# Edge values of raw patch sets moved to GpSimd, and a root spread by a matmul, at the start of a two-layer lookup convolution

## The chip, the cores and the metric

The kernel runs on one core of one Trainium2 chip. The metric is the device time of one execution in microseconds (us), lower is better; the time of a kernel is the median of its runs. Engines are named as in the profile: PE is TensorE (matmuls; PEld its weight loads), DVE VectorE, ACT ScalarE, POOL GpSimd, SP the engine whose queue issues most DMA transfers. "L489" is line 489 of the kernel before.

## The reference

The input x has 16 images of 256 channels of 28 x 28. It is group-normalised (32 groups of 8 channels, no scale or shift), goes through two lookup convolutions, each followed by an inference batch norm, then through a squeeze-and-excite gate, and is added back twice:

```python
def amm_conv3x3(x, centroids, w_sub, stride=1):
    B = x.shape[0]
    C, k, s = centroids.shape                      # 256, 16, 9
    patches = conv_general_dilated_patches(x, (3, 3), (1, 1), 'SAME')
    p = patches.reshape(B, C, s, Ho * Wo).transpose(0, 3, 1, 2)
    d = sum(p * p) - 2.0 * einsum('bncs,cks->bnck', p, centroids) + sum(centroids * centroids)
    attn = softmax(-d, axis=-1)
    lut = einsum('cks,cso->cko', centroids, w_sub)
    return einsum('bnck,cko->bno', attn, lut)

def _L0_conv_ref(x, ...):
    out = relu(bn_inference(amm_conv3x3(x, centroids1, wsub1), ...))
    out = bn_inference(amm_conv3x3(out, centroids2, wsub2), ...)
    out = se_layer(out, se_w1, se_b1, se_w2, se_b2)
    return relu(out + x)

x = x + _L0_conv_ref(_gn(x), ...)
```

Per channel, a 3x3 patch is compared with 16 centroids, and the softmax over the 16 weighs rows of a table. The convolution pads with zeros, and what is padded is the normalised image.

## The kernel before

The work is cut into 128 blocks: layer, image, and within an image four blocks of a channel half `hh` and an image half `t` (14 rows, 392 pixels), in the order (0,0), (0,1), (1,1), (1,0). A block does this: 64 logits matmuls (L578; 32 x 32 tiles) of two patch sets of 128 partitions x 8 x 392 into PSUM; exponentials on ACT (L589); sums of exponentials for the denominators by matmul (`num_b`, L643); a reciprocal on DVE (L671); numerators by matmul (`num_a`, L629); the reciprocals spread over partitions by shuffles on DVE (L682, L686); the scaling of the numerators, partly on DVE straight out of PSUM (L705), partly copied by ACT (L699) and scaled on POOL (L694). The four blocks of an image meet in a Strassen-like scheme: products of 9 matmuls of 128 x 128 (L713) over sums and differences of the scaled blocks, which POOL makes (`mix`, L720, L722), with weight sums made once at the start (L237). A ring of four double PSUM banks is shared by logits, sums, numerators and products.

The order on each engine is written by hand: `at(cl, sub, f)` puts a job at a key, the jobs are issued in the order of their keys, and each engine runs its instructions in that order. Where a set is loaded and where its edges are written is told by the tables `QUEUE` and `BORDER` (L63, L64), with one key for each of the eight sets of the first image.

The first image does not wait for its normalisation. Its first-layer patch sets are taken raw, cut out of x on the host (`p0`), and loaded by `raw` (L269 to L273), five transfers per set on SP's queue. Sets 1 and 2 belong to the first block and lie in `pts`; sets 3 and 4, of the second block, lie in space that later holds weights (`alts`, called `wall` in the profile), filled with ones first (for set 3 by POOL, L1459); sets 5, 6 and 7, 8 lie in `pts` again, so that each waits until the logits that read its buffer are done.

The normalisation is folded into the weights `wx` of these blocks instead. For half k of the channels: `raw_stats` takes the channel means and variances on DVE (L424, L425) and spreads them by a one-hot table, `hot_sb`, to 16 columns (L432); `raw_mean` averages them over groups by a matmul with a block-diagonal matrix (`gmat`, L436) and turns the 16 columns into one value per patch row by a matmul with a matrix of 1/8 (`eighth`, L437); `raw_dev` and `raw_var` do the same for the variance (L443 to L445, L449, L450); `raw_norm` adds epsilon and takes the inverse root as a power on POOL, over 16 columns (L473), and makes scale and shift factors of it on POOL (L474, L475). `raw_keep` takes the root once more as one column (L481), for the later residual. `tap_scale` (L397) and `tap_shift` (L405, L408) multiply and shift the weights by these factors. All this comes ahead of the first logits for half 0, and later for half 1.

A raw set has zeros where its patches reach outside the image, where raw values would need the mean, so that the normalised value is zero. `border` writes that by two operations on DVE: the left and right columns of each of 8 sub-images get a term added (14 rows x 2 columns x 8 = 224 elements, L489), and the top or bottom row (28 x 8 = 224 elements) is multiplied by a zero-or-one column and gets a term (L491), which keeps a corner from being counted twice:

```python
cols = v[:, :, :, 0 : W : W - 1]
nc.vector.tensor_tensor(cols, cols, view(tm, 8 * p, [...]), ALU.add)
row = v[:, :, (RT - 1) * t, :]
nc.vector.scalar_tensor_tensor(
    row, row, hot_sb[:, 20 + t : 21 + t], tm[:, 2 + t, 8 * p : 8 * p + 8]..., op0=ALU.mult, op1=ALU.add)
```

The logits of a set wait for its edges. In the first blocks these engines also make the group norm of image 1 (`gn_stats`, `gn_mean`, `gn_var`: DVE L424, L425, L503 to L526, POOL L311, L312, L528, L529), write it to a zeroed buffer (`xpads`, memset L1461) and out to memory (`home`, L547); save the first layer's weights (`keep_wd`, two transfers on POOL's queue, L411); zero the buffers for the second layer (`hpads`, L1507); and make the batch norm factors (`setup_bn`, key (6, 2.75): L311 and L312 on POOL, then L320 to L328 on DVE).

Of the kernel before, what the change touches and what calls it, by code (L numbers as in the profile page):

```python
# [12 lines left out]
ALU = mybir.AluOpType  # L13
# [4 lines left out]
P = 128  # L18
# [4 lines left out]
RT = 14  # L23
# [6 lines left out]
GN_EPS = 1e-5  # L30
# [58 lines left out]
def kernel(  # L89
# [55 lines left out]
    def bank(name, step=None, role=None, tag=None):  # L145
        return banks(name, step, role, tag)[:, 0, :]
# [4 lines left out]
    def view(t, off, dims):  # L151
        return bass.AP(t.tensor, t.offset + off, [list(d) for d in dims])
# [104 lines left out]
    def piece(n):  # L257
        used[0] += n
        return first[:, used[0] - n : used[0]]
# [167 lines left out]
    def raw_stats(k):  # L427
        gn_stats(0, k)
        rr = piece(48).rearrange("p (a n) -> p a n", a=3)
        mv = gst[0][1][:, k, :]  # L430
        for i in range(2):
# [8 lines left out]
    def raw_dev(k):  # L440
        ps, rr, mean = raws["ps", k], raws["rr", k], gst[0][1][:, k, 0:1]
        dv = piece(2)
        nc.vector.tensor_sub(dv[:, 0:1], ps[:, 0:1], mean)  # L443
        nc.vector.scalar_tensor_tensor(dv[:, 1:2], ps[:, 0:1], mean, dv[:, 0:1], op0=ALU.subtract, op1=ALU.mult)
        nc.vector.scalar_tensor_tensor(rr[:, 0], hot_sb[:, :16], dv[:, 1:2], rr[:, 2], op0=ALU.mult, op1=ALU.add)  # L445
        raws["dv", k] = dv

    def raw_var(k, ps):
        nc.tensor.matmul(ps[:, :16], lhsT=eighth, rhs=raws["rr", k][:, 0], start=True, stop=True)  # L449
        nc.tensor.matmul(ps[:, 16:17], lhsT=gmat, rhs=raws["dv", k][:, 1:2], start=True, stop=True)  # L450
        raws["pv", k] = ps

    def raw_means(k):
        ps = raws.pop(("ps", k))
        m2 = piece(16)
        nc.vector.tensor_scalar(m2, ps[:, 16:32], 2.0, None, op0=ALU.mult)
        term = piece(64).rearrange("p (a n) -> p a n", a=4)
        nc.vector.tensor_tensor(
            term, ps[:, 16:32].unsqueeze(1).to_broadcast([P, 4, 16]), hot_sb[:, 16:20].unsqueeze(2).to_broadcast([P, 4, 16]),
            ALU.mult,  # L460
        )
        gm = piece(2)
        nc.vector.tensor_copy(gm, ps[:, :2])
        raws["m2", k], raws["term", k], raws["gm", k] = m2, term, gm

    def raw_norm(k):
        ve = piece(18)
        ps = raws.pop(("pv", k))
        nc.vector.tensor_scalar(ve[:, :17], ps[:, :17], GN_EPS, None, op0=ALU.add)
# [3 lines left out]
        nc.gpsimd.tensor_tensor(sc, ve[:, :16], mhalf, ALU.pow)  # L473
        nc.gpsimd.tensor_scalar(scm, sc, hot_sb[:, 22:23], hot_sb[:, 23:24], op0=ALU.mult, op1=ALU.add)  # L474
        nc.gpsimd.tensor_tensor(ms, raws["m2", k], sc, ALU.mult)  # L475
        raws["scm", k], raws["ms", k], raws["ve", k] = scm, ms, ve

    def raw_keep(k):
        ve, gm = raws["ve", k], raws["gm", k]
        rstd, shift = (nrm[:, 0, i, k : k + 1] for i in (1, 2))  # L480
        nc.gpsimd.tensor_tensor(rstd, ve[:, 17:18], mhalf[:, :1], ALU.pow)  # L481
        nc.gpsimd.tensor_tensor(shift, gm[:, 0:1], rstd, ALU.mult)
        nc.gpsimd.tensor_scalar(shift, shift, -1.0, None, op0=ALU.mult)

    def border(u, p):
        v = flat(u["pt", p]).rearrange("p (s r w) -> p s r w", s=8, w=W)
        tm, t = raws["term", u["hh"]], u["t"]
        cols = v[:, :, :, 0 : W : W - 1]
        nc.vector.tensor_tensor(cols, cols, view(tm, 8 * p, [tm.ap[0], [1, 8], [0, RT], [16, 2]]), ALU.add)  # L489
        row = v[:, :, (RT - 1) * t, :]  # L490
        nc.vector.scalar_tensor_tensor(  # L491
            row, row, hot_sb[:, 20 + t : 21 + t], tm[:, 2 + t, 8 * p : 8 * p + 8].unsqueeze(2).to_broadcast([P, 8, W]),
            op0=ALU.mult, op1=ALU.add,
        )

    def gn_mean(b, k0=0, n=NB, step=None):
        st, mv = gst[b]
# [691 lines left out]
    def at(cl, sub, f, *a, **kw):  # L1189
        jobs.setdefault((cl, sub), []).append((f, a, kw))  # L1190
# [272 lines left out]
    mean_off(0, 0, 256)  # L1463
    tap_sum(0, 0, bank("tap", tag=0)[:, :256])
    sq_add(0, 1)
# [122 lines left out]
def _lay_out(inputs):  # L1588
# [34 lines left out]
    hot = np.zeros((P, 24), np.float32)  # L1623
    pad = np.zeros((ch, H + 2, W + 2), np.float32)
    pad[:, 1 : H + 1, 1 : W + 1] = x[0]
    p0 = np.zeros((2, 2, 2, 72, 8, RT, W), np.float32)
    for p in range(P):
        dy, dx = divmod(rows[p % 16], 3) if p % 16 in rows else (1, 1)
        hot[p, p >> 3] = 1.0
        hot[p, 16:20] = dx == 0, dx == 2, dy == 0, dy == 2  # L1630
        hot[p, 20:22] = dy != 0, dy != 2
        hot[p, 22:24] = p % 16 in rows, p % 16 not in rows
# [53 lines left out]
```

## Time and profile before

| | us |
|---|---|
| median of 3 runs | 2619.93 |
| lowest and highest of them | 2618.88, 2620.37 |
| the profiled execution's own time | 2617.88 |
| its span in the profile | 2616.4 |
| PE, DVE, ACT, POOL busy in it | 2591.2, 1786.9, 1368.6, 1900.2 |
| mean granted clock of PE | 0.998 |

How to read it: the page gives totals of one execution, the windows view cuts it into stretches, and the timeline lists instructions in order of time, each with the time that its engine sat idle before it and what ended that. Starts are counted from the beginning of the span. A time "busy" includes what an instruction spends blocked once it has begun.

### The profile page before, as it was taken

To read this page: it belongs to the slowest core of one execution; us is meant where nothing else is said; L and a number is where in the kernel's file an instruction comes from. 1 tells how busy PE (TensorE), PEld (TensorE's weight loads), DVE (VectorE), ACT (ScalarE), POOL (GpSimd) and SP (SyncE) were. 2 spreads that over 40 slices of the span, in tenths; PEclk is the share of its full clock that TensorE was granted. 3 is DMA by queue.
4 is the path that set the end of the run, shared out by engine and by line. 5 is a ranking of instruction groups with operands and counts; after the bars stand their busy time and mean duration, and the time that the engine had idled before them with its cause. 6 is when DMAs were issued, how large, how long until landed. Compare 5 with 4: busy or idle time off the path is not lost.

```text
span 2616.4 us, 85872 instructions
## 1 busy us (share of the span) xinstructions
PE 2591.2 (99%) x37026; PEld 1272.7 (49%) x37026; DVE 1786.9 (68%) x3812; ACT 1368.6 (52%) x1912; POOL 1900.2 (73%) x1323
## 2 busy tenths in 40 slices
PE   7999999999999999999999999999999999999999
PEld 3444454444444444444444444444444444444445
DVE  8776656666566665666666776767777667767676
ACT  5444444444444444444454655565555555555565
POOL 5786666766568766676667777778878788787776
PEclk9999999999999999999999999999999999999999
DMA  7566656665556565655664444444444444444442
GB/s 206 136 166 177 198 149 185 170 176 173 145 144 153 168 186 174 175 145 152 170 170 107 112 115 117 130 115 113 107 130 120 121 118 106 116 128 126 116 105 66
DMA packets 213672, 372.07 MB, mean 142 GB/s; under 512 B 29880, under 2 KB 183912, under 8 KB 212712
## 3 DMA queue, kind: packets, MB, share of 16 engines
q1 hardware_dynamic: 206968, 333.75, 48.0%
q0 software_dynamic: 6176, 32.66, 3.4%
q8 instruction: 295, 4.83, 0.8%
q14 instruction: 89, 0.73, 0.1%
q10 hardware_dynamic: 144, 0.10, 0.0%
HBM read 288.46 MB, written 77.95 MB: 140 GB/s over the span
## 4 chain that ended last, share of the span: by engine, by line
PE 98%; DVE 1%; issue 0%; ACT 0%; DMA 0%; POOL 0%; ACTq 0%; DVEq 0%; POOLq 0%
PE acc L713 52%; PE lg L578 17%; PE na L629 14%; PE nb L643 14%; ACT e L589 0%; PE sep L1014 0%; DMA pt<-in_p 0%; POOL qp L722 0%; PE sep L1006 0%; DVE rb L686 0%; DMA xt<-in_x 0%; PE tap L390 0%; PE sqp L374 0%; PE sqp L343 0%; DVE qp L705 0%
## 5 line engine op out<-in xcount | busy, mean ns | idle before, releaser
L713 PE MATMUL acc<-qp,wall 128*128 128x392 f32 (+1 forms) x3088 | 1100.1, 499 | 0.6 <-issue 0.3
L589 ACT ACTIVATE e<-lg 128x784 f32<-128x784 f32 x960 | 737.5, 821 | 644.2 <-PE lg L578 641.5
L722 POOL TENSOR_TENSOR qp<-qp,qp 128x784 f32<-128x784 f32 x512 | 943.7, 1866 | 159.6 <-DVE qp L705 159.2
L713 PEld LDWEIGHTS acc<-qp,wall 128*128 128x128 f32 x3088 | 569.6, 190 | 507.4 <-issue 59.5
L686 DVE STREAM_SHUFFLE rb<-r 128x392 f32<-128x392 f32 x1024 | 550.8, 604 | 0.0
L578 PE MATMUL lg<-pt,wd 32*32 32x392 f32 x15872 | 468.9, 499 | 1.0 <-issue 1.0
L657 DVE SCALAR_TENSOR_TENSOR r<-nb,kst,r 128x392 f32<-128x392 f32 x128 | 80.1, 626 | 446.2 <-ACT r L653 445.6
L705 DVE TENSOR_TENSOR qp<-na,rb 128x784 f32<-128x784 f32 x352 | 333.8, 972 | 61.2 <-PE na L629 50.0
L629 PE MATMUL na<-e,cwa 64*32 64x392 f32 x8192 | 374.1, 492 | 0.0
L643 PE MATMUL nb<-e,cwb 64*32 64x392 f32 x8192 | 373.5, 492 | 0.4 <-ACT e L589 0.3
L694 POOL TENSOR_TENSOR qo<-qo,rb 128x392 f32<-128x392 f32 x128 | 132.5, 1035 | 296.1 <-DVE rb L682 295.7
L671 DVE RECIPROCAL r<-r 128x392 f32<-128x392 f32 x128 | 333.2, 2603 | 4.4
L694 POOL TENSOR_TENSOR qp<-qp,rb 128x784 f32<-128x784 f32 x160 | 295.9, 1860 | 3.2 <-issue 0.4
L643 PEld LDWEIGHTS nb<-e,cwb 64*32 64x32 f32 x8192 | 189.4, 107 | 175.1 <-issue 21.1
L629 PEld LDWEIGHTS na<-e,cwa 64*32 64x32 f32 x8192 | 182.6, 106 | 182.5 <-issue 74.4
L578 PEld LDWEIGHTS lg<-pt,wd 32*32 32x32 f32 x15872 | 116.1, 103 | 266.1 <-issue 230.2
L713 PE MATMUL acc<-qp,w_A 128*128 128x392 f32 x512 | 183.9, 502 | 0.0
L653 ACT ACTIVATE r<-nb,kst 128x392 f32<-128x392 f32 x128 | 86.7, 677 | 166.2 <-PE nb L643 158.6
L613 POOL TENSOR_TENSOR z<-z,mx 128x1568 f32<-128x1568 f32 x32 | 91.8, 2870 | 94.8 <-DVE mx L607 94.8
L713 PE MATMUL acc<-qo,wall 128*128 128x392 f32 (+1 forms) x386 | 158.0, 491 | 0.0
L699 ACT COPY qp<-na 128x784 f32<-128x784 f32 x160 | 130.0, 813 | 21.7 <-PE na L629 20.2
L713 PEld LDWEIGHTS acc<-qp,w_A 128*128 128x128 f32 x512 | 95.3, 191 | 83.0 <-DVE qp L705 19.8
(229 smaller groups left out, 1706.8 us busy)
## 6 DMA issues: line engine op xcount, KB each, us to landing
pt<-home SPq DMA_DIRECT2D x744, 209.0 KB
pt<-home SPq DMA_DIRECT2D x744, 104.5 KB
home<-xpad SPq DMA_DIRECT2D x30, 899.0 KB
xt<-in_x SPq DMA_DIRECT2D x30, 784.0 KB
out_dram<-y SPq DMA_DIRECT2D x31, 392.0 KB
pt<-in_p SPq DMA_DIRECT2D x24, 196.0 KB
d_wS<-st SPq DMA_DIRECT2D x12, 192.0 KB
wall<-d_wS SPq DMA_DIRECT2D x4, 576.0 KB
```

The costliest lines, as they stand in the source:

```text
L578: nc.tensor.matmul(bk[32 * c : 32 * c + 32, :N].rearrange("p (r w) -> p r w", w=W), lhsT=(wx[u["hh"]] if early(u) else wts["wd", u["hh"]]) ...
L589: nc.scalar.activation(eg[:, 2 * i : 2 * i + 2, :], bk[:, :, :N], AF.Exp, scale=2.0)
L613: nc.gpsimd.tensor_tensor(zk, zk, mx.unsqueeze(2).to_broadcast([P, N // 4, K]), ALU.subtract)
L629: nc.tensor.matmul(bs[32 * i : 32 * i + 32, r, :N], lhsT=wts["cwa", u["hh"]][64 * r : 64 * r + 64, mm, i, :], rhs=es[64 * r : 64 * r + 64, ...
L643: nc.tensor.matmul(bs[32 * i : 32 * i + 32, r, :N], lhsT=wts["cwb", u["hh"]][64 * r : 64 * r + 64, mm, i, :], rhs=es[64 * r : 64 * r + 64, ...
L671: nc.vector.reciprocal(u["r"], u["r"])
L686: nc.vector.stream_shuffle(rb[:, r, :], u["r"], mask_of(2 * mm + r))
L694: nc.gpsimd.tensor_tensor(q, q, u.pop(("rb", mm)), ALU.mult)
L699: nc.scalar.copy(pair(u, mm), u.pop(("na", mm))[:, :, :N])
L705: nc.vector.tensor_mul(pair(u, mm), u.pop(("na", mm))[:, :, :N], rb)
L713: nc.tensor.matmul(accs[key][:, : cols[1] - cols[0]], lhsT=wl[w][:, k, :], rhs=us["q", k][:, cols[0] : cols[1]], start=first and n == 0, s ...
L722: nc.gpsimd.tensor_tensor(pair(out_u, mm), pair(in0, mm), pair(in1, mm), ALU.subtract)
```

## The change

Seven of the eight sets (all but set 1) get their edges on POOL, by three additions: the two columns over the 13 rows that are not the edge row (208 elements), the edge row without its ends (26 x 8 = 208), and the ends of that row (16), whose terms come from four new columns of `hot_sb` (28 columns in place of 24). The term table has 8 kinds instead of 4. Set 1 stays with two operations on DVE. The keys of `BORDER` change.

For half 0 the root is taken once, of one column: `raw_root` sends one column of variances through `gmat` (one matmul in place of two), adds the terms and epsilon on DVE and takes the power on POOL into `nrm`. `raw_scales` multiplies the one-hot table by that root on DVE and spreads it by a matmul with `eighth` to 16 columns, out of which DVE makes the factors that POOL made. `raw_keep` then has no power of its own for half 0. Half 1 keeps its way. `eighth` lies in space of the zeroed buffers `hpads`, whose memsets move from key (1, 1.95) to (3, 1.55); the memsets of `xpads` and `raw_keep` of half 0 move behind set 2's edges.

The transfer of set 7 is put at key (4, 0.35) in place of (4, 1.5), ahead of the first product.

```diff
-QUEUE = (None, None, (-0.9, 0.0), (-0.4, 0.0), (0, 1.5), (1, 1.5), (4, 1.5), (5, 1.5))
-BORDER = ((-0.5, 0.0), (-0.3, 0.0), (1, 0.97), (1, 1.9), (2, 1.6), (4, 0.5), (5, 1.1), (7, 0.2))
+QUEUE = (None, None, (-0.9, 0.0), (-0.4, 0.0), (0, 1.5), (1, 1.5), (4, 0.35), (5, 1.5))
+BORDER = ((-0.5, 0.0), (-0.3, 0.0), (1, 0.5), (1, 0.98), (2, 0.5), (3, 1.5), (4, 0.82), (6, 2.72))
...
-    eighth = piece(P)
+    eighth = hpads[1][:, :P]
...
+    def raw_root(ps):
+        ve, gm = piece(2), raws["gm", 0]
+        rr, rstd = raws["rr", 0], nrm[:, 0, 1, 0:1]
+        nc.tensor.matmul(ps[:, :1], lhsT=gmat, rhs=raws["dv", 0][:, 1:2], start=True, stop=True)
+        sq_add(0, 0)
+        nc.vector.scalar_tensor_tensor(ve[:, 0:1], ps[:, :1], GN_EPS, gm[:, 1:2], op0=ALU.add, op1=ALU.add)
+        nc.gpsimd.tensor_tensor(rstd, ve[:, 0:1], mhalf[:, :1], ALU.pow)
+
+    def raw_scales(ps):
+        rr, rstd = raws["rr", 0], nrm[:, 0, 1, 0:1]
+        nc.vector.tensor_scalar(rr[:, 0], hot_sb[:, :16], rstd, None, op0=ALU.mult)
+        nc.tensor.matmul(ps[:, 16:32], lhsT=eighth, rhs=rr[:, 0], start=True, stop=True)
+        sq_add(0, 1)
+        scm, ms = piece(16), piece(16)
+        nc.vector.tensor_scalar(scm, ps[:, 16:32], hot_sb[:, 26:27], hot_sb[:, 27:28], op0=ALU.mult, op1=ALU.add)
+        nc.vector.tensor_tensor(ms, ps[:, 16:32], raws["m2", 0], ALU.mult)
+        raws["scm", 0], raws["ms", 0] = scm, ms
...
     def border(u, p):
...
-        cols = v[:, :, :, 0 : W : W - 1]
-        nc.vector.tensor_tensor(cols, cols, view(tm, 8 * p, [tm.ap[0], [1, 8], [0, RT], [16, 2]]), ALU.add)
+        first = u["hh"] == 0 and t == 0 and p == 0
+        r0, r1 = (0, RT) if first else (1 - t, RT - t)
+        eng = nc.vector if first else nc.gpsimd
+        cols = v[:, :, r0:r1, 0 : W : W - 1]
+        eng.tensor_tensor(cols, cols, view(tm, 8 * p, [tm.ap[0], [1, 8], [0, r1 - r0], [16, 2]]), ALU.add)
         row = v[:, :, (RT - 1) * t, :]
...
+        eng.tensor_tensor(
+            row[:, :, 1 : W - 1], row[:, :, 1 : W - 1],
+            tm[:, 2 + t, 8 * p : 8 * p + 8].unsqueeze(2).to_broadcast([P, 8, W - 2]), ALU.add,
+        )
+        ends = row[:, :, 0 : W : W - 1]
+        eng.tensor_tensor(ends, ends, view(tm, 16 * (4 + 2 * t) + 8 * p, [tm.ap[0], [1, 8], [16, 2]]), ALU.add)
...
-    raw_var(0, bank("gnq", tag=3))
+    ps = bank("gnq", tag=3)
+    raw_root(ps)
+    nc.gpsimd.memset(alts[0], 1.0)
     sq_sum(0, 1, bank("sqp", tag=2)[:, :256])
     raw_means(0)
-    sq_add(0, 0)
-    raw_norm(0)
-    nc.gpsimd.memset(alts[0], 1.0)
-    for t in xpads:
-        nc.gpsimd.memset(t, 0.0)
-    raw_keep(0)
     mean_off(0, 0, 256)
+    raw_scales(ps)
...
+    for t in xpads:
+        at(-0.2, 0.0, nc.gpsimd.memset, t, 0.0)
+    at(-0.2, 0.1, raw_keep, 0)
...
     for t in hpads:
-        at(1, 1.95, nc.gpsimd.memset, t, 0.0)
+        at(3, 1.55, nc.gpsimd.memset, t, 0.0)
```

More of the change, by code (lines that the diff above doesn't have):

```diff
@@ L430, in raw_stats @@
         mv = gst[0][1][:, k, :]
-        for i in range(2):
+        for i in range(1 + k):
             nc.vector.tensor_scalar(rr[:, 1 + i], hot_sb[:, :16], mv[:, i : i + 1], None, op0=ALU.mult)
@@ L444, in raw_dev @@
         nc.vector.scalar_tensor_tensor(dv[:, 1:2], ps[:, 0:1], mean, dv[:, 0:1], op0=ALU.subtract, op1=ALU.mult)
-        nc.vector.scalar_tensor_tensor(rr[:, 0], hot_sb[:, :16], dv[:, 1:2], rr[:, 2], op0=ALU.mult, op1=ALU.add)
-        raws["dv", k] = dv
+        if k:
+            nc.vector.scalar_tensor_tensor(rr[:, 0], hot_sb[:, :16], dv[:, 1:2], rr[:, 2], op0=ALU.mult, op1=ALU.add)
+        gm = piece(2)
+        nc.vector.tensor_copy(gm, ps[:, :2])
+        raws["dv", k], raws["gm", k] = dv, gm
     def raw_var(k, ps):
@@ L473, in raw_norm @@
         nc.gpsimd.tensor_tensor(sc, ve[:, :16], mhalf, ALU.pow)
-        nc.gpsimd.tensor_scalar(scm, sc, hot_sb[:, 22:23], hot_sb[:, 23:24], op0=ALU.mult, op1=ALU.add)
+        nc.gpsimd.tensor_scalar(scm, sc, hot_sb[:, 26:27], hot_sb[:, 27:28], op0=ALU.mult, op1=ALU.add)
         nc.gpsimd.tensor_tensor(ms, raws["m2", k], sc, ALU.mult)
@@ L478, in raw_keep @@
     def raw_keep(k):
-        ve, gm = raws["ve", k], raws["gm", k]
+        gm = raws["gm", k]
         rstd, shift = (nrm[:, 0, i, k : k + 1] for i in (1, 2))
-        nc.gpsimd.tensor_tensor(rstd, ve[:, 17:18], mhalf[:, :1], ALU.pow)
+        if k:
+            nc.gpsimd.tensor_tensor(rstd, raws["ve", k][:, 17:18], mhalf[:, :1], ALU.pow)
         nc.gpsimd.tensor_tensor(shift, gm[:, 0:1], rstd, ALU.mult)
@@ L487, in border @@
         tm, t = raws["term", u["hh"]], u["t"]
[L488 to L494 removed]
+        first = u["hh"] == 0 and t == 0 and p == 0
[3 more added lines that the diff above has]
+        eng.tensor_tensor(cols, cols, view(tm, 8 * p, [tm.ap[0], [1, 8], [0, r1 - r0], [16, 2]]), ALU.add)
+        row = v[:, :, (RT - 1) * t, :]
+        if first:
+            nc.vector.scalar_tensor_tensor(
+                row, row, hot_sb[:, 24 + t : 25 + t], tm[:, 2 + t, 8 * p : 8 * p + 8].unsqueeze(2).to_broadcast([P, 8, W]),
+                op0=ALU.mult, op1=ALU.add,
+            )
+            return
+        eng.tensor_tensor(
+            row[:, :, 1 : W - 1], row[:, :, 1 : W - 1],
+            tm[:, 2 + t, 8 * p : 8 * p + 8].unsqueeze(2).to_broadcast([P, 8, W - 2]), ALU.add,
+        )
+        ends = row[:, :, 0 : W : W - 1]
+        eng.tensor_tensor(ends, ends, view(tm, 16 * (4 + 2 * t) + 8 * p, [tm.ap[0], [1, 8], [16, 2]]), ALU.add)
     def gn_mean(b, k0=0, n=NB, step=None):
@@ L1622, in _lay_out @@
     rows = {tap_row(s): s for s in range(S)}
-    hot = np.zeros((P, 24), np.float32)
+    hot = np.zeros((P, 28), np.float32)
     pad = np.zeros((ch, H + 2, W + 2), np.float32)
@@ L1630, in _lay_out @@
         hot[p, 16:20] = dx == 0, dx == 2, dy == 0, dy == 2
-        hot[p, 20:22] = dy != 0, dy != 2
-        hot[p, 22:24] = p % 16 in rows, p % 16 not in rows
+        hot[p, 20:24] = dx == 0 or dy == 0, dx == 2 or dy == 0, dx == 0 or dy == 2, dx == 2 or dy == 2
+        hot[p, 24:26] = dy != 0, dy != 2
+        hot[p, 26:28] = p % 16 in rows, p % 16 not in rows
     for n, p in enumerate(p for first, step in RAW for p in range(first, P, step)):
```

9 lines of the change are left out of this document (3 added, 6 removed).

## The prediction

> **What bounds the kernel now.** I read the page first, then the windows view, then the timeline of the first 80 us.
>
> ```profile
> span 2616.4 us, 85872 instructions
> PE 2591.2 (99%) x37026; PEld 1272.7 (49%) x37026; DVE 1786.9 (68%) x3812; ACT 1368.6 (52%) x1912; POOL 1900.2 (73%) x1323
> ```
>
> TensorE (PE) is the bound: 2591.2 of 2616.4 us. The windows (columns: length; busy of PE, its weight loads, DVE, ACT, POOL; granted clock; DMA share; GB/s) say where its 25 idle us are and where it runs at half clock.
>
> ```profile
> 0.00:20.00 20.00, 11.87 (x144) 6.00 (x144) 13.54 (x37) 11.81 (x11) 12.81 (x25) 1.00 0.88 227
> 20.00:40.00 20.00, 17.44 (x344) 7.39 (x336) 17.42 (x42) 10.84 (x15) 11.32 (x12) 1.00 0.98 233
> 40.00:65.00 25.00, 18.91 (x310) 8.78 (x311) 23.57 (x50) 10.46 (x14) 10.55 (x10) 0.93 0.54 169
> 65.00:130.00 65.00, 64.61 (x925) 30.90 (x897) 48.91 (x119) 28.82 (x40) 47.97 (x37) 0.95 0.53 137
> ...
> 44.77:48.19 3.42, 3.42 (x20) 1.51 (x5) 3.39 (x5) 1.51 (x2) 0.00 (x0) 0.50 0.42 123
> 65.25:72.08 6.83, 6.83 (x55) 2.90 (x38) 6.65 (x21) 3.53 (x5) 4.85 (x7) 0.50 0.50 152
> ```
>
> PE idles 8.13, 2.56 and 6.09 us in the first three windows and 0.39 in the fourth. Half a clock for 3.42 and 6.83 us loses 1.71 and 3.42 us of matmul time. All that this change touches lies here. Next, the gaps in the timeline (start, duration, engine, line, tiles; in brackets the idle time before):
>
> ```profile
> 14.44 4.00 PE L578 MATMUL lg<-pt,first 32*32 32x392 f32 x88 [2.37 <-issue]
> ...
> 25.25 0.54 DVE L489 TENSOR_TENSOR wall<-wall,first 128x224 f32<-128x224 f32 x1
> ...
> 26.38 0.63 PE L578 MATMUL lg<-wall,first 32*32 32x392 f32 x16 [0.82 <-issue]
> ...
> 33.35 0.62 PE L578 MATMUL lg<-wall,first 32*32 32x392 f32 x16 [1.00 <-ACT qp L699]
> ...
> 36.69 3.86 POOL L694 TENSOR_TENSOR qp<-qp,rb 128x784 f32<-128x784 f32 x2
> ...
> 37.44 1.54 DVE L489 TENSOR_TENSOR pt<-pt,first 128x224 f32<-128x224 f32 x1
> 39.01 1.80 DVE L491 SCALAR_TENSOR_TENSOR pt<-pt,hot_sb,first 128x224 f32<-128x224 f32 x1
> ...
> 42.21 1.81 PE L578 MATMUL lg<-pt,first 32*32 32x392 f32 x48 [2.35 <-issue]
> ...
> 58.17 4.80 POOL L722 TENSOR_TENSOR qp<-qp,qp 128x784 f32<-128x784 f32 x2
> ...
> 59.32 1.95 DVE L237 TENSOR_TENSOR wall<-wall 128x1152 f32<-128x1152 f32 x1
> ...
> 61.19 2.18 DVE L489 TENSOR_TENSOR pt<-pt,first 128x224 f32<-128x224 f32 x1
> 63.41 0.96 DVE L491 SCALAR_TENSOR_TENSOR pt<-pt,hot_sb,first 128x224 f32<-128x224 f32 x1
> ...
> 64.47 3.42 PE L578 MATMUL lg<-pt,first 32*32 32x392 f32 x64 [3.54 <-issue]
> ```
>
> The gaps before 26.38, 42.21 and 64.47 are logits that wait for DVE to write edge values (L489, L491) into sets 3, 5 and 7. For 5 and 7 those two operations are stretched while POOL works beside them: 1.54 and 2.18 us for L489, against 0.54 at 25.25. After the gaps of 2.35 and 3.54 us come the two half-clock stretches; after 0.82 and 1.00 us comes none.
>
> **The change, part by part.** Gains are counted at PE's next milestone, since later waits can eat an earlier gain.
>
> *The root of the first half.*
>
> ```profile
> 8.72 2.94 POOL L473 TENSOR_TENSOR first<-first,mhalf 128x16 f32<-128x16 f32 x1 [3.75 <-DVE first L469]
> ...
> 12.16 0.42 DVE L397 TENSOR_TENSOR first<-wd,first 128x256 f32<-128x256 f32 x1 [1.37 <-POOL first L474]
> ...
> 16.69 0.60 POOL L481 TENSOR_TENSOR nrm<-first,mhalf 128x1 f32<-128x1 f32 x1
> ```
>
> A 16-column power of 2.94 us becomes a 1-column one of 0.60. A matmul spreads the root to 16 columns and two small DVE operations replace POOL's two. The path cannot gain more than the 1.37 us that DVE's L397 waited: before that DVE is busy with the weights' means, which stay. The DVE operations that move in cost about 0.4 us of this. Gain at the first logits: 0.95 (bounds 0 and 1.37).
>
> *Edges of sets 2 to 8 on POOL.* Per set, two DVE operations go (0.55 and 0.45 us unhindered) and three POOL additions come: columns 208 elements, row 208, row ends 16.
>
> ```profile
> L720 POOL TENSOR_TENSOR qo<-qo,qo 128x392 f32<-128x392 f32 x4 | 4.1, 1028 | 0.1
> ...
> L757 POOL TENSOR_TENSOR hpad<-hpad,half_sum 128x392 f32<-128x392 f32 x2 | 1.9, 964 | 0.1
> ...
> L475 POOL TENSOR_TENSOR first<-first 128x16 f32<-128x16 f32 x2 | 0.4, 220 | 0.0
> ```
>
> In these groups (count, busy us, mean ns) POOL adds 392 elements in 1028 ns, also into a padded image (L757, 964), and 16 in 220. On that line 208 take 0.63, so a set takes about 1.5 us. No row shows POOL on columns 27 elements apart; bounds 0.5 and 2 us per addition. I take 0.63, nearest in size and kind.
> The Trainium skill ("GPSIMD Engine Reference", section 4.1, engine selection) speaks against the change: it puts elementwise additions on VectorE, with GpSimd about two times slower. The rows agree (1.5 against 1.0 us), and by the rule alone each set would become later; but the stretched rows show that a set cost DVE 3.3 us where it mattered.
>
> Set 3, bound by its transfer. It was whole by 25.25, when L489 ran without a wait; the queues were 0.98 full in 20 to 40 us, so an earlier issue brings nothing. I estimate 24.3, working from the DMA completions in the trace. With 1.5 us and a hop, its logits start at about 26.0 instead of 26.38, though PE is ready 0.9 earlier: the gain falls to 0.35.
> Set 4: its edges leave DVE, but PE waits there for ACT's copy; half of the 1.00 comes back. Gain at 36.99, where the sums of exponentials start: 0.85.
> Set 5: the two additions run on POOL ahead of its L694 pair, so neither is blocked. DVE still has the weights' shift behind it, about 0.75 us of the 2.35 stay. Gain: 0.85 + 1.6 + 0.75 (the two shift operations move up as well) = 3.2.
> Half clock at 44.77: with a gap of 0.75 it should not come, +1.7; less 0.6, as the next product then waits for DVE's statistics of image 1. Gain 4.3. DVE's scaling at 55.27 gains less than PE, because its seven shuffles stand before it: 3.7 at the end of the next sums (60.93).
> Set 7 runs on POOL before the L722 additions that stretched it. The 3.54 us go, and with them both half-clock windows: 3.7 + 3.5 + 3.4 = 10.6; I take 10.2 at the numerators (74.72), as their operands bind a little.
>
> *The seventh set's place in the queue.*
>
> ```profile
> 44.36 1.24 PE L578 MATMUL lg<-pt,first 32*32 32x392 f32 x16 [0.34 <-DVE qo L668]
> ...
> 45.65 3.05 SPq L272 DMA_DIRECT2D pt<-in_p  x5
> ```
>
> Its first transfer was issued at 45.65, right as the last logits that read the old buffer ended (45.60), and SP has no other transfer between the two places. Worth 0 by itself; it follows PE, which is earlier by 3.2.
>
> *What is late next.* POOL is now the queue with everything in it.
>
> ```profile
> 64.20 1.05 POOL L720 TENSOR_TENSOR qo<-qo,qo 128x392 f32<-128x392 f32 x1
> ...
> 65.22 1.84 POOL L722 TENSOR_TENSOR qp<-qp,qp 128x784 f32<-128x784 f32 x1
> ...
> 67.01 1.24 POOL L411 DMA_DIRECT2D d_wd<-wd x2
> ...
> 68.32 0.22 POOL L311 TENSOR_SCALAR rs_t<-vecs 128x2 f32<-128x2 f32 x1
> ...
> 68.62 0.72 POOL L312 TENSOR_TENSOR bnsc<-rs_t,mhalf 128x2 f32<-128x2 f32 x1
> ...
> 71.16 0.16 DVE L326 TENSOR_TENSOR bnsc<-bnsc,vecs 128x2 f32<-128x2 f32 x1
> ...
> 74.72 2.86 PE L629 MATMUL na<-e,cwa 64*32 64x392 f32 x64
> ...
> 75.72 0.97 DVE L705 TENSOR_TENSOR qp<-na,rb 128x784 f32<-128x784 f32 x1 [2.45 <-PE na L629]
> ...
> 77.52 1.00 PE L578 MATMUL lg<-pt,first 32*32 32x392 f32 x32
> ```
>
> POOL's stretch from L720 to the two L411 transfers, then L311 and L312 twice, feeds DVE's L326, which stands ahead of DVE's scaling (L705), whose release of a bank the logits at 77.52 need. POOL's work here moves only as far as DVE's L705 and L237 let it: I reckon the last L722 to end at 63.7, the transfers at 64.95, set 8's edges (1.5, now between) at 66.4, L312 at 68.45. L705 then starts at 68.95 instead of when the numerators come, and the logits start at 70.0, where PE is ready at 67.3. A new gap of 2.7 us: gain 7.5.
> Is it followed by half a clock? By rows: 2.35 us was, with one stretch of 3.42 us (1.7 lost), 1.00 was not. 2.7 is nearest the first, so I take 1.7. Gain 7.5 − 1.7 = 5.8.
> The Trainium skill ("TensorE: Matmul & The Clock Gate", "Why this matters for your kernels") allows gaps up to about 3 us and gives a window of 3.4 us. The 3.42 us stretch agrees with the window, the stretch after 2.35 us does not agree with the allowance; by that rule the gain would stay 7.5.
>
> Everything after 130 us is unchanged: PE's order is the same but for the small matmuls of the root. Sum against the profiled execution (2617.88 us, span 2616.4; 2 us under the median 2619.93): −5.8, so 2614.1 on the median.
>
> **Rivals.**
> *No half clock after the new gap:* gain 7.5, 2612.4. For it: 2.35 us brought one stretch of 3.42 and 3.54 us brought two, so two rows do not settle which gaps drop the clock; against it the row at 44.77.
> *The new wait does not bite,* because POOL's additions are shorter or L722 comes earlier than I reckon: gain 9 to 10.2, 2610. Against it: 1.5 us of edges and 3.2 us of transfers and roots stand in a row on POOL.
> *Little is left:* the gap of set 3 (24.75 to 25.95 by my count, 1.2 us) also brings half a clock, and edges cost 1 us per addition: set 3 is 0.75 later, set 8's chain 0.75 to 1.5 later. Gain 5.8 − 1.7 − 1.9 = 2.2, 2617.7: within 0.2% (5.2 us, about what a measurement here tells from no change).
> *Slower:* one mechanism, POOL's price for the strided columns and rows. At 2 us per addition a set takes 4.2 us: set 3's logits are 2.7 us later, set 8 puts 2.7 us on the new gap, sets 6 and 7, in a row with POOL's L694 and the group-norm chain, some 2.7 more; with the half clock after set 3's gap (1.7) that is 9.8 on a gain of 5.8: 2624. It turns to a loss above about 1.5 us per addition. Against it: L757 at 964 ns for 392 elements in rows of 28.
> *The earlier queue place does nothing,* as said; that is already in the sum.
>
> **How the numbers follow.** Gain 5.3 to 6.8 (my case) 0.30; no half clock 0.23; no new wait 0.11; little left 0.26; slower 0.10. Faster by over 0.2%: the first three, 0.64 less 0.04 for sizes, 0.60. Same 0.31; slower by over 0.2% 0.09. Below 2609.5 I leave 0.06, above 2619.5 0.12: the range reaches from the full gain to no gain at all. The likeliest's own range is 2612 to 2616.
>
> **What would show it.** Right: POOL additions of about 0.63 us (208) and 0.22 (16); PE's first logits at 13.5; no clock of 0.50 near 44; the gap before set 7's logits gone; a gap of 2 to 3 us near 67 to 70 whose chain runs over L312 and L326 of the old numbering, and one half-clock stretch behind it. Wrong: additions above 1 us, a set-3 gap above 2 us, half a clock before 35 us, or differences after 130 us.

## The result, and the profile after

In paired runs of both kernels the changed kernel takes 2614.30 us (median of 9, 2610.43 to 2616.80), the kernel before 2620.28 us (9 runs, 2618.88 to 2622.54): 6.0 us less, a ratio of 0.9978 with a 95% interval of 0.9968 to 0.9987. The forecast was 2614.1.

The traced execution of the changed kernel took 2616.80 us, the slowest of its nine; the traced one of before took 2617.88 us, faster than any of the nine above. So the two traces differ by 1.1 us in span only, and what they show is read at the start of the kernel, where the change is. Lines are numbered anew in the changed kernel: logits L609 (before L578), denominator sums L674 (L643), numerators L660 (L629), products L744 (L713), DVE's scaling L736 (L705), additions of scaled blocks on POOL L753 (L722).

The page and the windows view after (columns as in the prediction):

```profile
span 2615.3 us, 85874 instructions
PE 2592.6 (99%) x37026; PEld 1273.7 (49%) x37026; DVE 1782.9 (68%) x3798; ACT 1369.0 (52%) x1912; POOL 1908.4 (73%) x1341
...
0.00:20.00 20.00, 10.45 (x116) 5.83 (x119) 15.18 (x35) 10.49 (x9) 11.41 (x25) 1.00 0.88 233
20.00:40.00 20.00, 18.99 (x345) 7.46 (x340) 15.87 (x38) 12.48 (x17) 13.19 (x19) 0.91 0.96 239
40.00:65.00 25.00, 23.66 (x397) 10.47 (x382) 23.02 (x49) 13.92 (x19) 18.00 (x20) 1.00 0.53 167
65.00:130.00 65.00, 62.60 (x870) 30.36 (x869) 49.63 (x120) 28.64 (x39) 48.45 (x39) 0.97 0.57 145
...
36.52:39.94 3.42, 3.42 (x36) 1.37 (x42) 3.08 (x7) 0.71 (x1) 3.42 (x5) 0.50 0.96 245
74.07:77.48 3.41, 3.41 (x51) 1.32 (x65) 3.31 (x8) 0.97 (x2) 3.41 (x3) 0.50 0.02 5
```

PE idles 9.55, 1.01, 1.34 and 2.40 us in the four windows (before: 8.13, 2.56, 6.09, 0.39). It is worse before 20 us, much better from 20 to 65, and there is a new wait behind 65. Half-clock time fell from 10.25 to 6.83 us.

The timeline of the changed kernel, at the places that the prediction names:

```profile
8.24 0.58 POOL L473 TENSOR_TENSOR nrm<-first,mhalf 128x1 f32<-128x1 f32 x1 [3.28 <-DVE first L472]
8.79 2.89 POOL L1487 MEMSET wall<- 128x3360 f32 x1
...
9.07 2.64 DVE L477 TENSOR_SCALAR first<-hot_sb,nrm 128x16 f32<-128x16 f32 x1
...
11.77 0.61 PE L478 MATMUL gnq<-first,hpad 128*128 128x16 f32 x2 [2.92 <-DVE wd L379]
...
15.75 1.62 PE L609 MATMUL lg<-pt,first 32*32 32x392 f32 x32 [0.90 <-PE tap L390]
...
24.07 0.95 POOL L512 TENSOR_TENSOR wall<-wall,first 128x208 f32<-128x208 f32 x1 [4.43 <-DMA wall<-in_p]
25.10 0.54 POOL L520 TENSOR_TENSOR wall<-wall,first 128x208 f32<-128x208 f32 x1
25.59 0.25 POOL L525 TENSOR_TENSOR wall<-wall,first 128x16 f32<-128x16 f32 x1
...
26.80 2.77 PE L609 MATMUL lg<-wall,first 32*32 32x392 f32 x64
...
41.69 1.82 PE L609 MATMUL lg<-pt,first 32*32 32x392 f32 x48
...
59.91 2.77 PE L609 MATMUL lg<-pt,first 32*32 32x392 f32 x64
...
69.92 0.16 DVE L326 TENSOR_TENSOR bnsc<-bnsc,vecs 128x2 f32<-128x2 f32 x1 [1.31 <-POOL bnsc L312]
...
72.46 0.95 PE L609 MATMUL lg<-pt,first 32*32 32x392 f32 x32 [2.18 <-issue]
```

The waits before the logits of sets 3, 5 and 7 (26.80, 41.69 and 59.91; before 0.82, 2.35 and 3.54 us) are gone: no idle time is noted beside them. The first logits start at 15.75, 1.31 us later than before. And the new gap of 2.18 us stands at 72.46, where DVE's batch norm operation (L326) waits for POOL's root (L312).

A measure for the experiments that leaves out most of the run is the start of the fifth block's numerators, behind which both kernels do the same work; before and after, from the timeline:

```profile
114.66 1.60 PE L629 MATMUL na<-e,cwa 64*32 64x392 f32 x32
```

```profile
110.74 1.60 PE L660 MATMUL na<-e,cwa 64*32 64x392 f32 x32
```

3.92 us earlier in these two executions. How many stretches of half clock fall into the start differs from one execution to the next, though, so this number moves too. And the rest moves as well: from this point to the end of the span the same work took 2501.7 us before and 2504.6 after, and 2500.0 to 2505.3 in the fourteen traces of the table below. So the start of one trace and the timed total need not agree to better than some us.

### The profile page after: what moved, and what is told of

Its sections match the earlier page's. It is cut to its first block, busy times and chain, and to the rows that moved or that the text cites. A ratio compares the mean times of both kernels' runs of the same rounds, so it can differ in the third digit from the quotient of the medians.

```text
span 2615.3 us, 85874 instructions
## 1 busy us (share of the span) xinstructions
PE 2592.6 (99%) x37026; PEld 1273.7 (49%) x37026; DVE 1782.9 (68%) x3798; ACT 1369.0 (52%) x1912; POOL 1908.4 (73%) x1341
## 4 chain that ended last, share of the span: by engine, by line
PE 97%; DVE 1%; POOL 0%; issue 0%; ACT 0%; DMA 0%; SPq 0%; POOLq 0%; ACTq 0%
PE acc L744 52%; PE lg L609 17%; PE na L660 14%; PE nb L674 14%; ACT e L620 0%; DMA pt<-in_p 0%; DVE r L702 0%; PE sep L1045 0%; POOL qp L753 0%; PE sep L1037 0%; DMA xt<-in_x 0%; PE tap L390 0%; DVE rb L717 0%; DVE gn_st L424 0%; DVE qp L736 0%
## 5 line engine op out<-in xcount | busy, mean ns | idle before, releaser
L744 PE MATMUL acc<-qp,wall 128*128 128x392 f32 (+1 forms) x3088 | 1098.4, 499 | 1.7 <-DVE rb L713 1.4
L753 POOL TENSOR_TENSOR qp<-qp,qp 128x784 f32<-128x784 f32 x512 | 943.5, 1867 | 152.6 <-DVE qp L736 152.0
L744 PEld LDWEIGHTS acc<-qp,wall 128*128 128x128 f32 x3088 | 568.6, 190 | 505.3 <-issue 53.4
L609 PE MATMUL lg<-pt,wd 32*32 32x392 f32 x15872 | 468.7, 500 | 0.0
L674 PE MATMUL nb<-e,cwb 64*32 64x392 f32 x8192 | 375.9, 493 | 0.4 <-ACT e L620 0.2
L660 PE MATMUL na<-e,cwa 64*32 64x392 f32 x8192 | 375.1, 492 | 0.2 <-issue 0.2
L736 DVE TENSOR_TENSOR qp<-na,rb 128x784 f32<-128x784 f32 x352 | 333.8, 972 | 60.0 <-PE na L660 47.9
L674 PEld LDWEIGHTS nb<-e,cwb 64*32 64x32 f32 x8192 | 190.6, 107 | 176.7 <-issue 26.5
L660 PEld LDWEIGHTS na<-e,cwa 64*32 64x32 f32 x8192 | 183.5, 106 | 182.7 <-issue 74.3
L609 PEld LDWEIGHTS lg<-pt,wd 32*32 32x32 f32 x15872 | 116.6, 103 | 266.5 <-issue 238.3
L744 PE MATMUL acc<-qp,w_A 128*128 128x392 f32 x512 | 182.7, 499 | 0.0
L744 PE MATMUL acc<-qo,wall 128*128 128x392 f32 (+1 forms) x386 | 158.0, 491 | 0.0
L744 PEld LDWEIGHTS acc<-qp,w_A 128*128 128x128 f32 x512 | 94.6, 190 | 82.1 <-DVE qp L736 19.8
```

The lines of the kernel that those rows point to most:

```text
L609: nc.tensor.matmul(bk[32 * c : 32 * c + 32, :N].rearrange("p (r w) -> p r w", w=W), lhsT=(wx[u["hh"]] if early(u) else wts["wd", u["hh"]]) ...
L660: nc.tensor.matmul(bs[32 * i : 32 * i + 32, r, :N], lhsT=wts["cwa", u["hh"]][64 * r : 64 * r + 64, mm, i, :], rhs=es[64 * r : 64 * r + 64, ...
L674: nc.tensor.matmul(bs[32 * i : 32 * i + 32, r, :N], lhsT=wts["cwb", u["hh"]][64 * r : 64 * r + 64, mm, i, :], rhs=es[64 * r : 64 * r + 64, ...
L736: nc.vector.tensor_mul(pair(u, mm), u.pop(("na", mm))[:, :, :N], rb)
L744: nc.tensor.matmul(accs[key][:, : cols[1] - cols[0]], lhsT=wl[w][:, k, :], rhs=us["q", k][:, cols[0] : cols[1]], start=first and n == 0, s ...
L753: nc.gpsimd.tensor_tensor(pair(out_u, mm), pair(in0, mm), pair(in1, mm), ALU.subtract)
```

## The experiments

All twelve in one table. "First logits" and "fifth block" are starts in the one traced execution, "half clock" is the time at a granted clock of 0.50 between 20 and 100 us in it (the slow time before the first full clock is not in it); "difference" is the timed median minus that of the kernel before from the same set of runs, with the interval of the ratio.

| run | first logits | fifth block | half clock | difference | ratio, 95% |
|---|---|---|---|---|---|
| before | 14.44 | 114.66 | 10.25 | | |
| the change | 15.75 | 110.74 | 6.83 | −6.0 | 0.9968 to 0.9987 |
| stt | 13.34 | 109.35 | 0 | −5.6 | 0.9966 to 0.9984 |
| root_only | 17.41 | 117.74 | 13.65 | +3.1 | 1.0001 to 1.0019 |
| borders_only | 14.46 | 106.81 | 0 | −6.8 | 0.9964 to 0.9984 |
| bn_early | 15.81 | 110.39 | 6.83 | −5.9 | 0.9968 to 0.9988 |
| bn_late | 14.34 | 112.95 | 6.83 | −2.2 | 0.9984 to 1.0002 |
| stt_bn_late | 13.29 | 113.75 | 6.83 | −2.4 | 0.9978 to 0.9996 |
| queue_back | 15.69 | 108.51 | 0 | −5.1 | 0.9972 to 0.9990 |
| dve_places | 14.42 | 110.48 | 6.83 | −5.1 | 0.9971 to 0.9990 |
| mixed | 14.61 | 112.89 | 3.41 | −5.1 | 0.9969 to 0.9987 |
| borders_b | 14.39 | 108.25 | 3.41 | −5.4 | 0.9964 to 0.9986 |
| after_b | 16.52 | 110.20 | 3.41 | −6.3 | 0.9965 to 0.9985 |
| queue_old | 16.32 | 109.94 | 3.41 | −5.2 | 0.9970 to 0.9988 |

The intervals are some 5 us wide. They tell root_only (+3.1) from all the others but bn_late, whose interval just reaches into its own (1.0002 against 1.0001). They do not tell those between −5.1 and −6.8 from one another. The two near −2 lie between: the interval of stt_bn_late overlaps all of those. Of the four kernels that were timed together, though, they have the higher medians (bn_late 2614.66 and stt_bn_late 2614.44 us, queue_back 2611.68 and dve_places 2611.72), so it is likely, not certain, that they lose some 2 to 3 us.

**stt: the spreading of the root in another form**

```diff
-        nc.vector.tensor_scalar(rr[:, 0], hot_sb[:, :16], rstd, None, op0=ALU.mult)
+        nc.vector.scalar_tensor_tensor(
+            rr[:, 0], hot_sb[:, :16], rstd, hot_sb[:, :16], op0=ALU.mult, op1=ALU.mult
+        )
```

> The changed kernel, but the one-hot table times the root is taken as scalar_tensor_tensor (hot x root x hot, the same values) in place of a tensor_scalar. Theory A (DVE's tensor_scalar was held by POOL's memset of 2.89 us, as the trace of the changed kernel has it at 2.64 us for 16 elements): the form with two SBUF inputs is not held by a memset that reads nothing, takes 0.2 us, and the first logits start at 13.2 us instead of 15.75. Theory B (the longer chain of hops itself costs the time): they start at 15.5 or later. Behind it, by A, set 3's edges (ending 25.84, bound by their transfer) take over: PE is 0.85 us earlier at the second block's logits, and the whole is 0.5 to 1.5 us faster than the changed kernel, about 2613.3 against 2620.3 before; by B nothing changes.

```profile
8.78 2.89 POOL L1489 MEMSET wall<- 128x3360 f32 x1
9.06 0.23 DVE L477 SCALAR_TENSOR_TENSOR first<-hot_sb,nrm 128x16 f32<-128x16 f32 x1
...
13.34 3.30 PE L611 MATMUL lg<-pt,first 32*32 32x392 f32 x64 [0.92 <-PE tap L390]
...
17.13 3.31 PE L611 MATMUL lg<-pt,first 32*32 32x392 f32 x64 [0.49 <-POOL pt L527]
...
23.25 4.34 PE L676 MATMUL nb<-e,cwb 64*32 64x392 f32 x64
```

Theory A holds for the place: beside the same memset the same 16 elements take 0.23 us in place of 2.64, and the first logits start at 13.34 (13.2 expected). The total did not follow. PE now waits 0.49 us for set 2, and it ran on at the slow rate: the 64 matmuls of the sums at 23.25 took 4.34 us, against 2.86 in the changed kernel. In the clock record of the trace the full clock came at 26.30 us, in the changed kernel at 19.46.

**root_only: the new root alone, edges as before**

```diff
-QUEUE = (None, None, (-0.9, 0.0), (-0.4, 0.0), (0, 1.5), (1, 1.5), (4, 0.35), (5, 1.5))
-BORDER = ((-0.5, 0.0), (-0.3, 0.0), (1, 0.5), (1, 0.98), (2, 0.5), (3, 1.5), (4, 0.82), (6, 2.72))
+QUEUE = (None, None, (-0.9, 0.0), (-0.4, 0.0), (0, 1.5), (1, 1.5), (4, 1.5), (5, 1.5))
+BORDER = ((-0.5, 0.0), (-0.3, 0.0), (1, 0.97), (1, 1.9), (2, 1.6), (4, 0.5), (5, 1.1), (7, 0.2))
...
-        first = u["hh"] == 0 and t == 0 and p == 0
+        first = True
```

> The kernel before with the new root of half 0 alone; all edges stay on DVE at their old places, set 7 in its old place of the queue. Theory A (the root is a loss in itself): first logits at 15.7 (before 14.44), the same gaps of about 2.4 and 3.5 us before the logits of sets 5 and 7, total 0 to 1.3 us slower than before. Rival (the root brings part of the gain): 0.5 to 1 us faster than before, first logits before 14.

```profile
8.87 2.89 POOL L1487 MEMSET wall<- 128x3360 f32 x1
9.15 4.22 DVE L477 TENSOR_SCALAR first<-hot_sb,nrm 128x16 f32<-128x16 f32 x1
...
11.71 1.63 POOL L1537 MEMSET xpad<- 128x900 f32 x2
...
40.86 1.53 DVE L512 TENSOR_TENSOR pt<-pt,first 128x224 f32<-128x224 f32 x1
42.42 1.81 DVE L515 SCALAR_TENSOR_TENSOR pt<-pt,hot_sb,first 128x224 f32<-128x224 f32 x1
...
63.85 2.18 DVE L512 TENSOR_TENSOR pt<-pt,first 128x224 f32<-128x224 f32 x1
```

A loss of 3.1 us, more than the 0 to 1.3 expected. Here no edges stand between POOL's memsets, so L477 is held over all of them: 4.22 us, until 13.37, where the last memset ends (13.34). The hold follows POOL's memsets, not the chain of hops (the steps from engine to engine). The first logits start 2.97 us later than before. The loss need not be the hold alone, since this trace also has 3.4 us more half clock than before. Of the two gaps that were expected, the one before set 7's logits came (3.52 us); the one before set 5's was 0.64, since PE ran at half clock from 31.21 to 38.04 us and was later itself. And on their old places the edges of sets 5 and 7 are held as before (columns 1.53 and 2.18 us), although the memsets have moved.

**borders_only and borders_b: the edges on POOL with the old root, twice**

```diff
-    ps = bank("gnq", tag=3)
-    raw_root(ps)
-    nc.gpsimd.memset(alts[0], 1.0)
+    raw_var(0, bank("gnq", tag=3))
...
+    sq_add(0, 0)
+    raw_norm(0)
+    nc.gpsimd.memset(alts[0], 1.0)
...
-    raw_scales(ps)
```

> The changed kernel with the old root of half 0 (16 columns on POOL). Theory A: first logits near 14.3; set 3's logits then start where its edges end (about 26), 0.5 to 0.9 us earlier than in the changed kernel, and the whole is 0.5 to 1.3 us faster than the changed kernel, so the edges carry all of the gain. Rival (the root is needed for the gain): 2 us or more slower than the changed kernel.

> borders_only once more, in one batch with the changed kernel. By the two traces it starts the fifth block's numerators 3.9 us earlier than the changed kernel, of which 1.7 us is a half-clock stretch that falls by chance and 1.3 the later first logits: 1 to 2 us faster than after_b in the timed runs. Rival (the new root costs nothing in the end, since set 3's transfer decides): within 0.5 us.

−6.8 and −5.4 us, beside −6.0 and −6.3 for the changed kernel: the edges carry all of the gain that can be told, and the new root is not needed. The expected 1 to 2 us between borders_b and after_b were not seen. In borders_only's trace the fifth block starts 7.85 us earlier than before; that is an execution without a half-clock stretch.

**bn_early: the batch norm factors at 20 us**

```diff
-    at(6, 2.75, setup_bn)
+    at(0, 1.6, setup_bn)
```

> The changed kernel with the batch norm factors (two power chains on POOL, seven small operations on DVE) made at about 20 us, where both engines are idle, in place of behind set 8's edges. Theory A (the gap of 2.18 us before the logits at 72.46 is POOL's chain of transfers, set 8's edges and these roots, which DVE's scaling stands behind): the gap falls below 0.5 us, the half-clock stretch of 3.41 us behind it goes, and the numerators of the fifth block start 2 to 3.9 us earlier than in the changed kernel (110.74). Rival (the logits wait for set 8's edges or for the numerators themselves): the gap stays above 1.5 us, or only the 0.9 us between set 8's edges and the scaling comes back.

```profile
20.93 0.16 DVE L326 TENSOR_TENSOR bnsc<-bnsc,vecs 128x2 f32<-128x2 f32 x1 [3.38 <-POOL bnsc L312]
...
23.81 0.56 PE L436 MATMUL sqp<-gn_mv,gmat 128*128 128x2 f32 x2 [2.34 <-DVE gn_mv L425]
...
73.16 1.00 PE L609 MATMUL lg<-pt,first 32*32 32x392 f32 x32
```

The gap at 72 is gone: the logits at 73.16 have no idle time. So the wait was POOL's chain in front of DVE's scaling. But the wait only moved. At 20 us POOL is behind set 2's edges and the memsets, DVE stands 3.38 us for its root, the statistics behind it come late, and PE waits 2.34 us there (0.54 in the changed kernel), with 6.83 us of half clock from 22.67 on. The fifth block starts 0.35 us earlier than in the change, where 2 to 3.9 were expected. −5.9 us: no gain on the change.

**bn_late and stt_bn_late: the factors behind DVE's scalings**

```diff
-    at(6, 2.75, setup_bn)
+    at(7, 1.1, setup_bn)
```

bn_late has the old root as well, stt_bn_late the form of stt.

> The changed kernel with the old root of half 0, and the batch norm factors made right behind DVE's scalings of the third block instead of ahead of them. Theory A (DVE's scaling, standing behind factors that POOL makes last, opens the gap of 2.2 us at 67 to 72 us): the gap falls below 0.4 us, no wait takes its place, the numerators of the fifth block start 9.5 to 10.3 us earlier than before (114.66), against 7.85 without this step; about 9 us faster than before in the timed runs. Rival (the logits wait for set 8's edges or a bank from elsewhere): the gap stays above 1.5 us.

> The changed kernel with the scalar_tensor_tensor form of the root's spreading, and the batch norm factors behind the scalings as in bn_late. Theory A: the first logits at 13.3, the gap at 72 us gone. If the earlier first logits are worth nothing, because set 3's transfer (edges start at 24.1 to 24.4 in every run so far) decides, the total equals that of bn_late within 1 us apart from the clock: a later start of the full clock (26.30 in the run stt, 19 to 20 in the others) costs up to 3 us of it. Rival (the new root is worth its 1 us): 1 us faster than bn_late.

```profile
67.98 1.00 PE L609 MATMUL lg<-pt,first 32*32 32x392 f32 x32
...
69.19 5.47 POOL L753 TENSOR_TENSOR qp<-qp,qp 128x784 f32<-128x784 f32 x3
69.27 1.80 DVE L320 TENSOR_SCALAR nb_sb<-vecs 128x2 f32<-128x2 f32 x1
...
71.17 1.71 DVE L327 TENSOR_TENSOR bnsh<-vecs,bnsc 128x2 f32<-128x2 f32 x1
...
72.92 1.77 DVE L328 TENSOR_TENSOR bnsh<-vecs,bnsh 128x2 f32<-128x2 f32 x1
...
77.15 1.56 PE L609 MATMUL lg<-pt,wd 32*32 32x392 f32 x16 [4.70 <-DVE half_sum L781]
```

For bn_late about −9 us were expected and −2.2 measured; stt_bn_late, at −2.4, lies within 1 us of it, as expected. The gap at 67 to 72 us is gone, as theory A has it, though POOL's edges and roots still stand where they stood; so it was DVE's scaling behind the factors that opened it. But a larger gap takes its place, and "no wait takes its place" was wrong. Three of DVE's operations on 128 x 2 elements now run beside POOL's additions and last 1.7 to 1.8 us, each as long as one addition. The shuffles and half_sum (L781) behind them are late, and PE waits 4.70 us for a bank, with 6.83 us of half clock from 75.78 on.

**queue_back and queue_old: the transfer of set 7 in its old place**

```diff
-QUEUE = (None, None, (-0.9, 0.0), (-0.4, 0.0), (0, 1.5), (1, 1.5), (4, 0.35), (5, 1.5))
+QUEUE = (None, None, (-0.9, 0.0), (-0.4, 0.0), (0, 1.5), (1, 1.5), (4, 1.5), (5, 1.5))
```

queue_old has this and set 7's edges at (4, 1.55) in place of (4, 0.82).

> The changed kernel with set 7's transfer back at its old place, behind the first product. As predicted: the order of SP's queue is the same, so no difference; within 1 us of the changed kernel (6.0 faster than before) and set 7's edges at the same distance from the last logits that read the buffer. Rival (the place matters): 1.5 us or more slower than the changed kernel.

> The changed kernel with set 7's transfer at its old place and set 7's edges right behind it, after the group norm chain on POOL (in queue_back the edges came ahead of the transfer, so that set 7 had none, and its transfer waited for them). As predicted for the place in the queue alone: the first transfer of set 7 is issued right as the logits that read its buffer end, as in the changed kernel (0.1 us behind them), and the total is within 0.7 us of after_b. Rival: it is issued 2 us or more behind them, and 1 us or more is lost.

In queue_back the edges are issued ahead of the transfer. They are added to what the buffer held, the transfer waits 4.3 us for them (issue at 48.15), and set 7 itself is left without edges; so it is no test of the place. queue_old is one: the first transfer is issued at 44.46, when the wait for the logits ends, and it takes −5.2 us beside −6.3 for after_b, 1.2 apart where 0.7 were expected, far inside the intervals. The fifth block starts 0.26 us earlier than in after_b. So the place is worth nothing by itself that these runs can tell, but edges as early as (4, 0.82) need the transfer ahead of them.

**dve_places and mixed: the new places, with the engine changed back**

```diff
-        first = u["hh"] == 0 and t == 0 and p == 0
+        first = True
```

dve_places has the old root and this; mixed has the old root and DVE for set 1 and sets 5 to 8 alone.

> The kernel before (old root) with all edges on DVE, but at the new places in the order. Theory A (the gain is from the engine): on DVE the early places make DVE wait for the transfers of sets 3, 4 and 7 with the reciprocal, the statistics and the shuffles behind them; slower than borders_only by 5 us or more, about as slow as before or slower. Rival (the gain is from the places): within 2 us of borders_only (6.8 faster than before).

> Old root of half 0; the new places for all edges; sets 2, 3 and 4 on POOL (where DVE would wait for transfers in dve_places), sets 5 to 8 on DVE (where POOL's chain is long). Theory P (the places give the gain, the engine only decides who waits): the gap near 67 us falls from 2.24 us (borders_only) to about 0.8 (dve_places), the gap of 1.75 us at 27.55 of dve_places is gone, and in the trace the numerators of the fifth block start about 9 us earlier than before where no half-clock stretch falls in, 1 to 1.5 us earlier than in borders_only; in the timed runs 0.5 to 1.5 us faster than borders_b. Rival (sets 5 and 7 need POOL): their edges on DVE are stretched beside POOL's work as in the kernel before (1.5 us or more for the columns), and it is 2 us or more slower than borders_b.

The groups of dve_places, by line (durations in ns: least, median, most):

```profile
L512 DVE TENSOR_TENSOR pt<-pt,first x6: 550/553/564, 13.3 to 69.7; 128x224 f32<-128x224 f32 x6
L512 DVE TENSOR_TENSOR wall<-wall,first x2: 555/556/557, 23.9 to 28.1; 128x224 f32<-128x224 f32 x2
its engine sat idle before it (us, times) until:
  DMA wall<-in_p: 5.3, 2
```

Theory A (the engine makes the gain) fell. With every edge on DVE, at the new places, the kernel is 5.1 us faster than before. No column operation took over 0.564 us, where before the slowest took 2.18. DVE does wait for transfers (5.3 us for sets 3 and 4), and a gap of 1.75 us before set 4's logits follows, but the gap of 3.5 us before set 7's logits is gone and the one near 72 us is 0.75, since set 8's edges are off POOL's chain. mixed was to take the best of both: the gap near 72 us (75.0 here) is 0.75 as expected, yet −5.1, no better, and the fifth block starts 1.77 us earlier than before where about 9 were expected without half clock (3.41 us of it fell in). In its trace DVE's scaling of the first block, with set 5's edges now ahead of it, leaves PE waiting 1.89 us at 35.8.

The new places that dve_places keeps are the keys of the edges, the key of set 7's transfer and the moved memsets. queue_old shows nothing for the second, and in root_only, which has the third and the old keys, the edges of sets 5 and 7 are still held; that leaves the keys of the edges. No run has the edges on POOL at the old keys, so what the engine would do alone is not shown.

**after_b: the change again**

> The changed kernel once more, unchanged, as the yardstick of this batch: 5 to 7 us faster than before. Its trace tells which of the half-clock stretches of the first trace (36.52 and 74.07 us) come again: the one behind the gap of 2.2 us if the gap brings it, either or neither if it hangs on how the stretches of 3.41 us happen to lie.

−6.3 us. Here the stretch behind the gap of 2.18 us comes again (71.75, below) and the one at 36.52 does not.

```profile
71.75:75.16 3.41, 3.41 (x35) 1.44 (x36) 3.16 (x8) 1.54 (x2) 3.41 (x2) 0.50 0.04 16
```

## Why the prediction was right, and where it was not

The total was right (−5.8 forecast, −6.0 and −6.3 measured), in part by luck: in the first trace every milestone falls short of the forecast. The numerators of the third block start 7.30 us early where 10.2 were forecast, the logits behind the new gap 5.06 (72.46 against 77.52) where 7.5 were, and at the fifth block 3.92 are left where 5.8 were. Two steps were wrong.

*The root: wrong in sign.* "Gain at the first logits: 0.95 (bounds 0 and 1.37)" measured −1.31, outside its bounds. I bounded a gain and allowed no loss, and priced the moved DVE operations by their lengths alone. What failed is the step "The DVE operations that move in cost about 0.4 us of this": the memset for set 3 now follows the power directly, L477 stood beside it, and alone took 2.64 us. stt shows the cause (0.23 in place of 2.64 us, and 13.34) and root_only shows it stronger (4.22 us, and 17.41). The Trainium skill ("SBUF — State Buffer", section "Who interferes with whom") says that a VectorE tensor_scalar can run in a mode that needs the ports shared with GpSimd, and then waits for whatever GpSimd instruction holds them, while an operation with two SBUF inputs contends only with a GpSimd instruction that reads. The trace agrees on both counts: 2.64 and 4.22 us against 0.23 beside a memset, and 1.71 us for a two-input operation beside POOL's additions in bn_late. The error cost less than 1.31, because before the change PE stood 0.82 us for set 3 at its next milestone, and now it comes there late and does not wait: at set 3's logits the change is 0.42 us behind (26.80 against 26.38) where I had it 0.35 ahead. With the old root the same logits start at 25.86 (borders_only). The edges of set 3 start with its transfer, at 24.07 (24.3 predicted).

*What the edges gained: right in size, wrong in cause.* In borders_only, which has the old root and no half-clock stretch, the third block's logits (set 5) start 3.34 us early (38.87 against 42.21; 3.2 predicted) and the numerators of the third block 10.14 us early (10.2 predicted; 64.58 against 74.72). In the first trace of the change the same numerators are 7.30 early: of the 2.84 us between the two traces 0.94 are there at set 3's logits, with the later first logits, and 1.7 are the half clock at 36.52, which no gap that I named explains. I put the gain to POOL ("the two additions run on POOL ahead of its L694 pair, so neither is blocked", "a set cost DVE 3.3 us where it mattered"). The first of these names the earlier place too ("ahead of"), but I priced the engine. dve_places shows that the place suffices: at the new keys DVE's own operations are not held either.

*The price on POOL.* 0.63 us for 208 elements was half right: the row additions take 0.53 to 0.72, the columns 27 elements apart 0.95 to 1.14, the ends 0.24 to 0.29. A set costs about 1.65 to 1.85 us in place of 1.5. The slower rival (a loss above 1.5 us an addition) was not near.

*The new wait: right.* Predicted 2.7 us at 67.3 to 70.0, through L312 and L326; measured 2.18 at 70.28 to 72.46, on that chain, and bn_early and bn_late take it away.

*The half clock behind it: right in this trace, not a rule.* A gap of 2.16 to 2.52 us at this place brought a stretch of 3.41 us in the change, after_b, queue_old and borders_b, and none in stt, borders_only and queue_back: four of seven. So the rival "no half clock" is as real as my case. The Trainium skill ("TensorE: Matmul & The Clock Gate", section "Why this matters for your kernels") allows gaps of up to about 3 us; the four cases disagree with it, the three agree. The traces hold a candidate for what parts them. Up to 100 us, the clock changes in each trace only at whole steps of 3.41 us, counted from the first full clock. In the four, one such step holds 1.80 to 2.18 us of PE's idle time; in the three the gap lies across the end of a step, and none holds more than 1.54. But idle time in a step does not sort the other cases (in the kernel before, a step with 1.50 us idle from 37.95 on was not followed by half clock and the next, with 1.19, was; in the first trace of the change 0.42 came ahead of 36.52), so this is not shown to be the rule. These stretches can make only part of the 6 us between the fastest and the slowest run of the changed kernel: 0 to 6.83 us of half clock are 0 to 3.4 us, and behind the start the same work varies by 5 us from trace to trace. No run isolates either.

*The queue place: right* (worth 0 as far as these runs can tell), but I missed that the early edges need it.

*What stays open.* Half-clock time in the traced starts is 10.25 us before and 0 to 6.83 in the runs between −5 and −7, so in these executions the clock makes 1.7 to 5.1 us of what the start gained (half of the difference), and the waits the rest; one execution for each does not settle the shares, and the time up to the first full clock, which also moved, is not counted in them. Whether the root in its stt form is worth anything at all, and whether POOL or DVE is better by less than 2 us, is below what these runs can tell. No version tried beats the changed kernel beyond its interval.

## What to carry to other kernels

When an operation moves to another engine and to another place in the order at once, run the new place on the old engine: here the place did the work. Before you price a short VectorE instruction by its length, look at what GpSimd runs beside it: here one of 128 x 2 elements took as long as the GpSimd addition that it met (1.71 us), and one of 128 x 16 took 2.64 us beside a memset in one form and 0.23 in another. A wait taken from the start of a pipeline is worth only what the next transfer or chain leaves of it; look for that before pricing the step.

## What the runs showed of the hardware that was not expected

- A tensor_scalar of 128 x 16 on DVE lasted 2.64 us beside a POOL memset and 4.22 us beside three in a row; a scalar_tensor_tensor of the same data beside the same memset took 0.23 us.
- The first grant of the full clock moved by up to 8.8 us between these kernels (17.47 to 26.30 us). In the three executions in which the logits of sets 1 and 2 were parted by 0.32 to 0.82 us (stt, stt_bn_late, mixed) it came at 25.2 to 26.3; in the others at 17.5 to 21.9. That is an observation on one execution each; the cause was not tried.
- In the first trace of the change the clock fell to half at 36.52 us, with no idle time of PE over 0.6 us in the 14 us before.
